# A one-core perceiver block: reordering the stretch behind the cross attention

## The chip, the cores and the metric

The kernel runs on one core of a Trainium2 chip. The metric is the device time of one execution in microseconds (us); the figure for a version is the median of several runs. The core's engines work side by side, each through its own list of instructions in order, and wait for each other through semaphores: PE multiplies matrices (PEld is its loading of weights), DVE does element-wise work and reductions, ACT does activation functions and copies, POOL does general work and issues some transfers, and SP only issues transfers. Transfers run on 16 DMA engines.

## What is computed

x has 2 batches of 512 tokens with 512 features; the context has 2 batches of 8192 tokens. Three residual blocks follow each other, each on a layer norm of its input:

```python
x = x + xattn(layernorm(x), ctx)     # 16 heads of 32, 8192 context tokens, output product Wo
x = x + window_attn(layernorm(x))    # 16 heads of 32, windows of 7 tokens, product W_proj
h = layernorm(x)                     # 1024 tokens
scores = sigmoid(h @ gate_w.T)       # 16 experts
topk_score, topk_ids = top_k(scores.T, 128)      # each expert picks its 128 best tokens
eo = silu(h[ids] @ gw.T + gb) * (h[ids] @ up_w.T + up_b)      # 2048 wide, by expert
eo = (eo @ down_w.T + down_b) * topk_score
shared = (silu(h @ sh_gate_w.T) * (h @ sh_up_w.T)) @ sh_down_w.T     # 1024 wide
x = x + shared + scatter_add(eo, ids)
```

Everything is in float32, except for some bias and mask factors that are split into three bfloat16 parts.

## The kernel before

Tokens lie in eight tiles of 128 rows (`n` 0 to 7; `b` is the batch, four tiles each). The residual x stays in `x_sb` for the whole kernel. A tile framework places instructions on each engine in an order that it chooses near the program's own, and adds the semaphores. A tile of a pool has a fixed number of buffers (`bufs`); a new tile of the same tag waits until the buffer's last readers are done. Pools opened in a `with` block give their memory back at its end, and a pool opened later in the same place waits for the last user of that memory.

Three stages matter here.

**Cross attention.** A loop over 146 slots handles chunks of 512 context tokens. `load` (SP) brings a chunk into one of four `ctx_t` buffers one slot ahead. In the last two slots only `scores` and `values` are left; there the running sum `acc` over the exponentials is added on DVE (L316). Behind the loop, `finish` for the last group sums `acc` on PE (`sm`, L324), takes the reciprocal (L330) and scales into `qT` on POOL (L332). Then `proj_residual` multiplies by Wo for each token tile (`po`, L92) and DVE adds bias and residual (`prt` L96, `x_sb` L97).

**Window attention.** SP loads three 1 MB tiles of `wqkv` and one of `wproj` into a pool of nine (`load_tile`, L371). `layernorm_stats` takes the statistics of all eight token tiles (L68, L69), then a square root on ACT (L71) and a reciprocal; each tile is normalized (`xn`, L77), transposed on PE (`tp`, L85) and copied by ACT into `xnT` (L86). After this, 8 groups (batch, four heads) of five query blocks run as a software pipeline of 40 items: `softmaxed` of one item, one of five `pieces` for the next group (`project` for k, `latent_k`, `project` for q, for v, `latent_v`), then `turned`, `weighed` and `placed` of the items before. A batch's last item is followed by `proj_residual` with W_proj for its four tiles.

**Feed-forward.** Behind that stand, in program order: `pick`, a selector of expert rows (three casts, L582); statistics, normalization, the write of each tile of h to memory (`h_dram`, on SP's queue, L602), transposes into `hT`; the gate product `pg` (L610) and its sigmoid; the selection, 16 rounds of `max`, `max_index` and `match_replace` on DVE (L624 to L627), eight tokens per expert and round; the splitting of the biases into three bfloat16 parts (`raw`, `part`, `bias3`, L641 to L645); and the shared expert, per batch 8 pairs of products `pf` (L658) with silu on ACT and a multiplication into `sT` on DVE (L665), then four products `pso` (L669) and the residual (L674). Then the selected tokens' numbers are transposed (`pt`, L679), `gather` fetches the first expert's tokens from `h_dram` by an indirect transfer on POOL's queue (L687), and 16 experts stream 12 MB of weights each through the nine-tile pool (`pf` L704, `py` L722).

Of the kernel before, what the change touches and what calls it, by code (L numbers as in the profile page):

```python
# [43 lines left out]
def perceiver_kernel(  # L44
# [18 lines left out]
    def layernorm_stats(pool):  # L63

        mv = pool.tile([P, NT, 2], F32, name="mv")
        for n in range(NT):
            st = pool.tile([P, 6], F32, name="st")
            nc.vector.bn_stats(out=st, in_=x_sb[:, n, :])  # L68
            nc.vector.bn_aggr(out=mv[:, n, :], in_=st)  # L69
        sd = pool.tile([P, NT], F32, name="sd")  # L70
        nc.scalar.activation(sd, mv[:, :, 1], AF.Sqrt, bias=eps)  # L71
        rs = pool.tile([P, NT], F32, name="rs")
        nc.vector.reciprocal(rs, sd)
        return mv, rs
# [13 lines left out]
    def proj_residual(aT, w_sb, b_bc, n, ps, pool):  # L88

        po = ps.tile([P, D], F32, tag="ps", name="po")  # L90
        for c in range(DC):
            nc.tensor.matmul(  # L92
                po, lhsT=aT[:, c, ts(n, P)], rhs=w_sb[:, c, :], start=(c == 0), stop=(c == DC - 1)
            )
        t = pool.tile([P, D], F32, tag="row", name="prt")
        nc.vector.tensor_tensor(t, po, b_bc, ALU.add)  # L96
        nc.vector.tensor_tensor(x_sb[:, n, :], x_sb[:, n, :], t, ALU.add)  # L97
# [5 lines left out]
    with ExitStack() as es:  # L103
        cp = es.enter_context(tc.tile_pool(name="a_const", bufs=1))
        tmp = es.enter_context(tc.tile_pool(name="a_tmp", bufs=2))
        ctxp = es.enter_context(tc.tile_pool(name="a_ctx", bufs=4))
# [229 lines left out]
        for slot in range(NS + LAG):  # L336
            if slot + 1 < NS + NKC:
                load(slot + 1)
            s = slot - LAG
# [17 lines left out]
        for i in range(4):  # L357
            finish(len(units) - 1, i)

        wo_sb = load_w(wo, ctxp, "ctx")  # L360
        bo_b = cp.tile([P, D], F32, tag="bv_b", name="bo_b")
        nc.gpsimd.dma_start(out=bo_b, in_=bo.partition_broadcast(P))
        for n in range(NT):
            proj_residual(qT, wo_sb, bo_b, n, ps, tmp)


    wpool = ctx.enter_context(tc.tile_pool(name="w", bufs=9))

    def load_tile(src):
        t = wpool.tile([P, 4, 512], F32, tag="w", name="wt")  # L370
        nc.sync.dma_start(out=t, in_=src)  # L371
        return t


    with ExitStack() as es:
# [3 lines left out]
        ps = es.enter_context(tc.tile_pool(name="b_ps", bufs=8, space=PSUM))  # L379

        wqkv_t = [
            load_tile(wqkv[:, ts(i, D)].rearrange("(c p) f -> p c f", p=P)) for i in range(3)
        ]
        wproj_sb = load_tile(wproj.rearrange("(c p) f -> p c f", p=P))
        bqkv_c = cp.tile([P, 12], F32, name="bqkv_c")
# [25 lines left out]
        xnT = cp.tile([P, DC, T], F32, name="xnT")  # L411
        mv, rs = layernorm_stats(tmp)
        for n in range(NT):
            xn = tmp.tile([P, D], F32, tag="row", name="xn")
            normalized(xn, n, mv, rs)
            transposed(xnT[:, :, ts(n, P)], xn, ps)

        aT = cp.tile([P, G, T], F32, name="aT")
# [8 lines left out]
        def project(i, which):  # L427
# [5 lines left out]
            for c in range(DC):  # L433
                nc.tensor.matmul(  # L434
                    pq, lhsT=wqkv_t[which][:, c, ts(g, P)], rhs=xnT[:, c, ts(b, S)],
# [105 lines left out]
        def placed(i, n):  # L541
# [6 lines left out]
            nc.scalar.copy(aT[:, g, ds(b * S + q0, nq)], tp[:, 0:nq])  # L548
            if g == G - 1 and n == NBQ - 1:
                for m in range(NT // B):  # L550
                    proj_residual(aT, wproj_sb, bproj_b, b * (NT // B) + m, ps, tmp)
# [4 lines left out]
        ]  # L556
        for f in pieces:
            f(0)
# [9 lines left out]


    cp = ctx.enter_context(tc.tile_pool(name="c_const", bufs=1))  # L570
    tmp = ctx.enter_context(tc.tile_pool(name="c_tmp", bufs=2))
    ps = ctx.enter_context(tc.tile_pool(name="c_ps", bufs=8, space=PSUM))
    dram = ctx.enter_context(tc.tile_pool(name="c_dram", bufs=1, space=bass.MemoryType.DRAM))
    h_dram = dram.tile([T, D], F32, name="h_dram")
# [3 lines left out]
    KB3 = 96  # L578
    pick = cp.tile([KB3, E, P], BF16, name="pick")
    for i in range(3):  # L580
        r = ds(32 * i, 32)
        nc.vector.tensor_copy(  # L582
            pick[r], ident[r, ds(32 * i, E)].unsqueeze(2).to_broadcast([32, E, P])
        )
    FB = 2 * F + D
    bias3 = cp.tile([KB3, FB], BF16, name="bias3")

    gate_sb = cp.tile([P, DC, E], F32, name="gate_sb")
    nc.gpsimd.dma_start(out=gate_sb, in_=gate.rearrange("(c p) e -> p c e", p=P))
    idx = cp.tile([P, E], U32, name="idx")  # L590
    scol = cp.tile([P, E], F32, name="scol")

    with ExitStack() as es:
        sp = es.enter_context(tc.tile_pool(name="s_const", bufs=1))
        st = es.enter_context(tc.tile_pool(name="s_tmp", bufs=2))

        hT = sp.tile([P, DC, T], F32, name="hT")
        mv, rs = layernorm_stats(st)
        for n in range(NT):
            h = st.tile([P, D], F32, name="h")  # L600
            normalized(h, n, mv, rs)
            nc.sync.dma_start(out=h_dram[ts(n, P), :], in_=h)  # L602
            transposed(hT[:, :, ts(n, P)], h, ps)


        sc = sp.tile([E, T], F32, name="sc")
        for i in range(T // 512):
            pg = ps.tile([P, 512], F32, tag="ps", name="pg")
            for c in range(DC):
                nc.tensor.matmul(  # L610
                    pg[0:E, :], lhsT=gate_sb[:, c, :], rhs=hT[:, c, ts(i, 512)],
                    start=(c == 0), stop=(c == DC - 1),
                )
            nc.scalar.activation(sc[:, ts(i, 512)], pg[0:E, :], AF.Sigmoid)
# [3 lines left out]
        work = [sp.tile([E, T], F32, tag=f"work{i}", name="work") for i in range(2)]  # L618
        top = sp.tile([E, CAP], F32, name="top")
        top_i = sp.tile([E, CAP], U32, name="top_i")  # L620
        cur = sc
        for i in range(CAP // 8):
            m8 = top[:, ts(i, 8)]
            nc.vector.max(out=m8, in_=cur)  # L624
            nc.vector.max_index(out=top_i[:, ts(i, 8)], in_max=m8, in_values=cur)
            if i < CAP // 8 - 1:
                nc.vector.match_replace(  # L627
                    out=work[i % 2], in_to_replace=m8, in_values=cur, imm_value=-1.0
                )
                cur = work[i % 2]  # L630
        top_f = sp.tile([E, CAP], F32, name="top_f")
        nc.vector.tensor_copy(top_f, top_i)

        raw = sp.tile([KB3, FB], F32, name="raw")
        nc.gpsimd.memset(raw, 0.0)
        for i in range(3):
            for src, lo, n in ((gb, 0, F), (up_b, F, F), (down_b, 2 * F, D)):
                nc.scalar.dma_start(out=raw[ds(32 * i, E), ds(lo, n)], in_=src)
        part = sp.tile([KB3, FB], BF16, name="part")
        for i in range(3):  # L640
            nc.vector.tensor_copy(part, raw)  # L641
            r = ds(32 * i, 32)
            nc.vector.tensor_copy(bias3[r], part[r])
            if i < 2:
                nc.vector.tensor_tensor(raw, raw, part, ALU.subtract)  # L645


        shg = [load_tile(sh_g[i]) for i in range(2)]
        shu = [load_tile(sh_u[i]) for i in range(2)]
        shd = [load_tile(sh_d[i]) for i in range(2)]  # L650
        for i in range(T // 512):
            sT = sp.tile([P, SH // P, 512], F32, tag="sT", name="sT")
            for f in range(SH // P):
                pair = []
                for wts in (shg, shu):
                    pf = ps.tile([P, 512], F32, tag="ps", name="pf")
                    for c in range(DC):
                        nc.tensor.matmul(  # L658
                            pf, lhsT=wts[f // 4][:, c, ts(f % 4, P)], rhs=hT[:, c, ts(i, 512)],
                            start=(c == 0), stop=(c == DC - 1),  # L660
                        )
                    pair.append(pf)
                sg = st.tile([P, 512], F32, name="sg")
                nc.scalar.activation(sg, pair[0], AF.Silu)
                nc.vector.tensor_tensor(sT[:, f, :], pair[1], sg, ALU.mult)  # L665
            for j in range(4):
                po = ps.tile([P, D], F32, tag="ps", name="pso")
                for f in range(SH // P):
                    nc.tensor.matmul(  # L669
                        po, lhsT=sT[:, f, ts(j, P)], rhs=shd[f // 4][:, f % 4, :],  # L670
                        start=(f == 0), stop=(f == SH // P - 1),
                    )
                n = i * 4 + j
                nc.vector.tensor_tensor(x_sb[:, n, :], x_sb[:, n, :], po, ALU.add)  # L674
                nc.sync.dma_start(out=out[ts(n, P), :], in_=x_sb[:, n, :])

        for src, dst in ((top_f, idx), (top, scol)):
# [130 lines left out]
```

## Time and profile before

| | |
|---|---|
| median of 3 runs | 3922.88 us (3919.61 to 3925.23) |
| the profiled execution | 3923.6 us, of which its span in the trace 3921.8 us |
| PE busy | 3822.6 us, 97% of the span |
| DVE busy | 2314.8 us, 59% |
| ACT busy | 1586.1 us, 40% |
| POOL busy | 2059.3 us, 53% |
| DMA, mean | 112 GB/s |

The stages in the trace, in us from the span's start: cross attention ends with its last `av` product at about 2704.5; Wo and the preparation of the window attention last until the first `plv` product (L472) at 2764.1; the window attention's last W_proj product ends at 2963.1; the shared expert's last product ends at 3171.9; the first expert begins at 3178.9.

How to read the views: in the slices a digit is a busy share in tenths, and the row PEclk is the clock that PE was granted, in tenths of full speed. A chain of waits gives start, length and the work or wait that held up the end. In a table of windows each engine has its busy time and, in brackets, its number of instructions; behind them stand the granted clock, the DMA share and GB/s. A row of the timeline has start, length, engine, line, operation, operands and, in square brackets, the idle time before it and what ended it.

### The profile page before, as it was taken

What the parts mean: (1) busy time and instruction counts of PE and PEld (TensorE: products, weight loads), DVE (VectorE), ACT (ScalarE), POOL (GpSimd) and SP (SyncE); (2) the same over time, 40 slices, a digit from 0 to 9 for tenths busy, and PEclk for the clock granted to TensorE, in tenths of its full rate; (3) what the DMA queues carried; (4) which work ended last, traced back from release to release, by engine and by line L of the source; (5) the groups of instructions that cost most, each with busy time, mean ns of one, the idle gap of its engine ahead of it and who ended that gap; (6) DMA issues with size and microseconds to landing.
All of it is one profiled execution on the core that took longest, in us unless ns stands there. A gap on an engine that the chain in (4) does not pass through costs nothing.

```text
span 3921.8 us, 99604 instructions
## 1 busy us (share of the span) xinstructions
PE 3822.6 (97%) x42828; PEld 1891.4 (48%) x42828; DVE 2314.8 (59%) x5833; ACT 1586.1 (40%) x2799; POOL 2059.3 (53%) x512
## 2 busy tenths in 40 slices
PE   7999999999999999999999999999997999999999
PEld 3445554554554554555555455444563444444444
DVE  4887777777777777777777777898346400000000
ACT  1005555555555555555555555675441001111110
POOL 0008998998998998999899899300000000000000
PEclk9889999999999999999999999999997999999999
DMA  4322222222223442222222222220201058888885
GB/s 157 95 84 71 70 70 66 69 69 69 69 69 106 125 125 92 69 69 69 69 69 69 69 69 66 66 85 26 81 33 42 32 203 286 288 288 288 283 285 178
DMA packets 144154, 440.29 MB, mean 112 GB/s; under 512 B 9312, under 2 KB 9456, under 8 KB 118272
## 3 DMA queue, kind: packets, MB, share of 16 engines
q1 hardware_dynamic: 139152, 423.72, 32.9%
q0 software_dynamic: 4272, 9.32, 1.0%
q8 instruction: 335, 5.49, 0.6%
q10 hardware_dynamic: 288, 0.89, 0.1%
q14 instruction: 107, 0.88, 0.1%
HBM read 425.44 MB, written 8.45 MB: 111 GB/s over the span
## 4 chain that ended last, share of the span: by engine, by line
PE 86%; DVE 3%; issue 2%; ACT 1%; DMA 1%; POOLq 0%; DVEq 0%; SPq 0%; ACTq 0%
PE av L304 12%; PE sx L246 12%; PE sc L282 11%; PE pv L226 11%; PE pf L704 11%; PE pk L210 10%; PE py L722 5%; PE sc L288 3%; PE pqkv L434 2%; PE pf L658 2%; PE po L92 1%; PE pso L669 1%; DVE junk L251 1%; PE pow L529 1%; PE tp L85 1%
## 5 line engine op out<-in xcount | busy, mean ns | idle before, releaser
L316 POOL TENSOR_TENSOR acc<-acc,pt 128x2048 f32<-128x2048 f32 x437 | 1992.1, 4558 | 483.9 <-ACT pt L295 482.7
L251 DVE CUSTOM_DVE_ANT_0 junk<-sx,mk 128x512 bf16<-128x512 f32 x2048 | 1416.2, 692 | 610.8 <-PE sx L246 378.1
L295 ACT ACTIVATE pt<-sc,mbias 128x512 f32<-128x512 f32 x2016 | 1218.5, 689 | 952.9 <-PE sc L288 951.4
L246 PE MATMUL sx<-kt,qT 32*128 32x512 f32 x4096 | 651.8, 645 | 0.6 <-ACT kt L214 0.6
L282 PE MATMUL sc<-qT,kt 32*128 32x512 f32 x4096 | 546.7, 594 | 0.0
L304 PE MATMUL av<-pt,vt 128*32 128x512 f32 x4032 | 540.5, 605 | 2.8 <-DVE mst L251 2.8
L226 PEld LDWEIGHTS pv<-wv_sb,ctx_t 128*32 128x32 f32 x16384 | 457.5, 110 | 155.5 <-DVE mst L251 104.4
L210 PE MATMUL pk<-ctx_t,wk_sb 128*32 128x256 f32 x8192 | 506.2, 389 | 2.1 <-DVE mst L251 2.1
L226 PE MATMUL pv<-wv_sb,ctx_t 128*32 128x128 f32 x16384 | 495.0, 273 | 1.3 <-DVE avs L312 1.3
L704 PE MATMUL pf<-wt,xinT 128*128 128x512 f32 x1024 | 461.0, 595 | 1.1
L210 PEld LDWEIGHTS pk<-ctx_t,wk_sb 128*32 128x32 f32 x8192 | 265.7, 112 | 309.0 <-DVE mst L251 133.6
L312 DVE TENSOR_TENSOR avs<-av,avs 128x512 f32<-128x512 f32 x504 | 345.3, 685 | 2.8 <-PE av L304 2.5
L282 PEld LDWEIGHTS sc<-qT,kt 32*128 32x128 f32 x4096 | 245.6, 184 | 202.0 <-issue 160.1
L711 DVE TENSOR_TENSOR eo<-pf,sg 128x512 f32<-128x512 f32 x64 | 44.3, 692 | 468.9 <-PE pf L704 461.9
L704 PEld LDWEIGHTS pf<-wt,xinT 128*128 128x128 f32 x1024 | 193.6, 190 | 222.4 <-issue 214.0
L246 PEld LDWEIGHTS sx<-kt,qT 32*128 32x128 f32 x4096 | 190.6, 185 | 211.4 <-DVE mst L251 159.7
L687 POOL DMA_INDIRECT xin<-h_dram,idx x16 | 15.9, 994 | 496.8 <-PE tp L85 291.7
L728 POOL DMA_INDIRECT out_x<-y,idx x16 | 25.3, 1580 | 408.8 <-DVE y L727 408.8
L304 PEld LDWEIGHTS av<-pt,vt 128*32 128x32 f32 x4032 | 81.6, 108 | 325.9 <-DVE mst L251 281.0
L214 ACT ACTIVATE kt<-pk,bk_c 128x256 f32<-128x256 f32 x256 | 121.2, 473 | 275.0 <-PE pk L210 274.9
L722 PE MATMUL py<-wt,eoT 128*128 128x512 f32 x512 | 222.4, 592 | 0.0
L709 ACT ACTIVATE sg<-pf 128x512 f32<-128x512 f32 x64 | 38.2, 597 | 422.2 <-PE pf L704 422.2
(152 smaller groups left out, 2276.9 us busy)
## 6 DMA issues: line engine op xcount, KB each, us to landing
ctx_t<-in_ctxT SPq DMA_DIRECT2D x160, 1024.0 KB, 6.5
wt<-in_gw SPq DMA_DIRECT2D x64, 1024.0 KB, 5.0
wt<-in_up SPq DMA_DIRECT2D x64, 1024.0 KB, 4.9
wt<-in_down SPq DMA_DIRECT2D x64, 1024.0 KB, 6.6
mk<-mrow SPq DMA_DIRECT2D x128, 256.0 KB, 3.5
wt<-in_wqkv SPq DMA_DIRECT2D x3, 1024.0 KB, 10.4
x_sb<-in_x SPq DMA_DIRECT2D x1, 2048.0 KB, 10.6
wt<-in_sh_g SPq DMA_DIRECT2D x2, 1024.0 KB, 15.1
```

The lines of the kernel that those rows point to most:

```text
L210: nc.tensor.matmul(pk[ts(h, DK), :], lhsT=wk_sb[:, c, ds(g * P + h * DK, DK)], rhs=ctx_t[slot, b][:, c, hs], start=(c == 0), stop=(c == DC ...
L214: nc.scalar.activation(k_t[slot][:, hs], pk, AF.Identity, bias=bk_c[:, g : g + 1])
L226: nc.tensor.matmul(pv[ts(k, DK), i, :], lhsT=ctx_t[slot, b][:, c, ds((2 * half + i) * P + k * DK, DK)], rhs=wv_sb[:, c, ts(g, P)], start=( ...
L246: nc.tensor.matmul(sm, lhsT=qT[r, g, ds(b * S + c * P, P)], rhs=k_t[s][r, :], start=True, stop=True)
L251: nc.vector.tensor_tensor_reduce(out=junk, in0=ss[h], in1=mk_t[s], scale=1.0, scalar=-3.0e38, op0=ALU.add, op1=ALU.max, accum_out=mst[u][: ...
L282: nc.tensor.matmul(sc, lhsT=k_t[s][r, ts(ch, P)], rhs=qT[r, g, ts(b, S)], start=True, stop=False)
L295: nc.scalar.activation(pt[:, h, :], ss[h], AF.Exp, bias=mbias[:, b, cc : cc + 1], scale=SCALE)
L304: nc.tensor.matmul(av[ts(h, DK), :], lhsT=v_t[s][:, ch, ts(h, DK)], rhs=pt_t[s, ch][:, h, :], start=True, stop=True,)
L312: nc.vector.tensor_tensor(avs[u], av, avs[u], ALU.add)
L316: eng.tensor_tensor(acc[u], acc[u], pt_t[s, ch], ALU.add)
L704: nc.tensor.matmul(pf, lhsT=xinT[:, c, :], rhs=wt[:, c, :], start=False, stop=(c == DC - 1))
L722: nc.tensor.matmul(py, lhsT=eoT[:, fq * 4 + c, :], rhs=wt[:, c, :], start=False, stop=(fq == FQ - 1 and c == 3),)
```

## The change

The four-buffer pool of the context chunks (`ctxp`) is opened at the top and lives to the end. In slot 143, the last one that uses a context chunk, SP also loads Wo and the three `wqkv` tiles into its buffers. The nine-tile weight pool becomes those four buffers and a pool of five, taken in turn by a counter; `wproj` and four tiles of the shared expert are requested ahead of the window attention, two more after it.

`finish` of the last group is called after the second Wo tile. `layernorm_stats` takes a range of tokens. The first batch's statistics follow its four Wo tiles, and only its four tiles are transposed before the window attention starts; the second batch's statistics and transposes, the three casts of `pick`, the splitting of the biases (in three loads of up to 2048 columns), and the first batch's layer norm and transposes for the feed-forward are put beside single items of the window attention's pipeline (`at`). `xnT`, `aT` and `hT` become tiles by batch in a pool of three. The writes of `h_dram` and the loads of `raw` go through POOL's queue, which before were SP's and ACT's.

In the shared expert, the second batch's layer norm and transposes stand behind products 1 to 4 of the first batch, the gate products behind product 5, and a round of the selection behind each later product (two behind each `pso`). The transposes `pt` and the gather stay at the end.

```diff
+    ctxp = ctx.enter_context(tc.tile_pool(name="ctx", bufs=4))
+    lnp = ctx.enter_context(tc.tile_pool(name="ln", bufs=2))
-    def layernorm_stats(pool):
+    def layernorm_stats(pool, tokens=range(NT)):
...
-        ctxp = es.enter_context(tc.tile_pool(name="a_ctx", bufs=4))
...
             if slot + 1 < NS + NKC:
                 load(slot + 1)
+            elif slot + 1 == NS + NKC:
+                wo_sb = load_w(wo, ctxp, "ctx")
+                wqkv_t = [load_w(wqkv[:, ts(i, D)], ctxp, "ctx") for i in range(3)]
...
         values(*waiting)
-        for i in range(4):
-            finish(len(units) - 1, i)
-
-        wo_sb = load_w(wo, ctxp, "ctx")
...
         for n in range(NT):
             proj_residual(qT, wo_sb, bo_b, n, ps, tmp)
+            if n == 1:
+                for i in range(4):
+                    finish(len(units) - 1, i)
+            if n == NT // B - 1:
+                ln_b0 = layernorm_stats(lnp, range(NT // B))
-    wpool = ctx.enter_context(tc.tile_pool(name="w", bufs=9))
+    wpool = ctx.enter_context(tc.tile_pool(name="w", bufs=5))
+    loads = [4]
 
     def load_tile(src):
-        t = wpool.tile([P, 4, 512], F32, tag="w", name="wt")
+        pool, tag = ((ctxp, "ctx"), (wpool, "w"))[loads[0] % 9 >= 4]
+        loads[0] += 1
+        t = pool.tile([P, 4, 512], F32, tag=tag, name="wt")
         nc.sync.dma_start(out=t, in_=src)
         return t
...
+        def bias_in(src, n):
+            raw = bp.tile([KB3, F], F32, name="raw")
+            nc.gpsimd.memset(raw, 0.0)
+            for i in range(3):
+                nc.gpsimd.dma_start(out=raw[ds(32 * i, E), 0:n], in_=src)
+            raws.append(raw)
+
+        def bias_part(i, lo, n):
+            raw = raws[-1]
+            part = bp.tile([KB3, F], BF16, name="part")
+            nc.vector.tensor_copy(part[:, 0:n], raw[:, 0:n])
+            r = ds(32 * i, 32)
+            nc.vector.tensor_copy(bias3[r, ds(lo, n)], part[r, 0:n])
+            if i < 2:
+                nc.vector.tensor_tensor(raw[:, 0:n], raw[:, 0:n], part[:, 0:n], ALU.subtract)
+
+        def forward_in(n, key):
+
+            b, m = divmod(n, NT // B)
+            if m == 0:
+                hT[b] = batch_tile("hT")
+            h = ctmp.tile([P, D], F32, name="h")
+            normalized(h, n, *lns[key])
+            nc.gpsimd.dma_start(out=h_dram[ts(n, P), :], in_=h)
+            transposed(hT[b][:, :, ts(m, P)], h, ps)
+
+        lns, raws = {"b0": ln_b0}, []
+        at(2, norm, 1, "b1")
+        for i, k in enumerate((4, 6, 8, 10)):
+            at(k, lambda n: attention_in(n, lns["b1"]), NT // B + i)
+        for i in range(3):
+            at(3 + 2 * i, picks, i)
+        k = 9
+        for src, lo, n in ((gb, 0, F), (up_b, F, F), (down_b, 2 * F, D)):
+            at(k, bias_in, src, n)
+            for i in range(3):
+                k += 2
+                at(k, bias_part, i, lo, n)
+        at(29, norm, 0, "f0")
+        for i, k in enumerate((31, 33, 35, 37)):
+            at(k, forward_in, i, "f0")
+        for n in range(NT // B):
+            attention_in(n, ln_b0)
         for f in pieces:
             f(0)
         for k in range(len(items) + 3):
...
+            for f in beside.get(k, ()):
+                f()
...
+    norm(1, "f1")
+    for b in range(B):
...
+            if b == 0 and 1 <= f <= 4:
+                forward_in(NT // B + f - 1, "f1")
+            elif b == 0 and f == 5:
+                gated(0)
+                gated(1)
+            elif b == 1 or f > 5:
+                select()
+        for j in range(4):
...
+            select()
+            select()
```

## What the prediction was, before the result

> **What bounds the kernel now.** I read the slices of the page first: they say where PE, busy for 97% of the span, is not.
>
> ```profile
> PE   7999999999999999999999999999997999999999
> DVE  4887777777777777777777777898346400000000
> PEclk9889999999999999999999999999997999999999
> ```
>
> PE dips, with its clock, in slice 30 of 40; the stretch that the change touches begins in slice 27, where DVE too is disturbed. So the second view is the chain of waits over that stretch.
>
> ```profile
> 2708.78 27.68 PE po L92 x64
> 2737.31 0.59 DVE x_sb L97
> 2738.44 10.36 DMA wt<-in_wqkv
> 2748.94 5.38 PE pqkv L434 x8
> ...
> 2964.47 5.47 DVE pick L582
> ...
> 2985.18 9.03 PE pg L610 x16
> ...
> 3037.87 0.61 DVE sT L665
> ...
> 3089.50 54.93 PE pf L658 x128
> 3144.43 27.47 PE pso L669 x64
> 3172.14 6.72 issue
> ```
>
> Work of PE is left four times here: for the `wqkv` load, for DVE ahead of `pg`, for one `sT` product on DVE, and at the end for the gather. Third, the windows of these stages, for idle time and clock.
>
> ```profile
> 2704.50:2764.10 59.60, 48.18 (x131) 22.27 (x130) 30.75 (x54) 9.78 (x16) 8.37 (x18) 0.94 0.43 156
> 2764.10:2861.10 97.00, 95.83 (x632) 61.03 (x633) 37.68 (x291) 53.62 (x153) 0.54 (x4) 1.00 0.02 6
> 2926.00:2963.10 37.10, 35.01 (x150) 22.62 (x148) 14.55 (x70) 10.30 (x34) 0.00 (x0) 0.68 0.00 0
> ...
> 2963.10:2974.60 11.50, 0.00 (x0) 0.00 (x0) 10.93 (x10) 1.58 (x2) 4.74 (x2) 0.60 0.36 117
> 2974.60:2985.10 10.50, 8.16 (x32) 6.00 (x32) 3.64 (x7) 4.10 (x7) 0.00 (x0) 0.50 0.59 203
> ...
> 3028.70:3038.50 9.80, 0.03 (x1) 0.00 (x0) 9.74 (x12) 0.00 (x0) 0.00 (x0) 0.75 0.00 0
> ```
>
> The window attention (second row) is PE's: 95.8 of 97 us, at full clock, DVE 39% busy, ACT 55%. Behind it PE has nothing for 11.5 us, then transposes at half clock for 10.5 us, and later nothing for 9.8 us.
>
> Last, single durations from the timeline.
>
> ```profile
> 2923.97 0.54 PE L517 MATMUL tpw<-ident,sb 103*109 103x103 f32 x4
> 2931.64 1.06 PE L517 MATMUL tpw<-ident,sb 103*109 103x103 f32 x4
> ...
> 2964.47 7.93 DVE L582 CAST pick<-ident 32x2048 bf16<-32x2048 f32 x3
> 2969.31 1.28 ACT L71 ACT_TABLE_LOAD   x1 [22.17 <-POOL raw L635]
> ...
> 3009.58 4.93 DVE L645 TENSOR_TENSOR raw<-raw,part 96x4608 f32<-96x4608 f32 x1
> ```
>
> Four transposes take 0.54 us at full and 1.06 us at half clock. The three casts of `pick` are 7.9 us of DVE.
>
> **The change part by part.** The order is that of the changed kernel's built lists of instructions; up to the last `av` and from the first expert on, PE's list is the old one.
>
> *A. Wo to the first group.* Before, PE waits from 2704.5 to 2707.7 for the last `acc`, and after `po` (to 2736.5) 12.4 us pass with transposes and two waits until `pqkv` at 2748.9. Now PE has two `po` tiles, `sm`, six `po` tiles, 16 transposes (of batch 0 only), `pqkv`. `po` can start at 2704.5 and ends after 27.7 + 1.1 (`sm`) at 2733.3. The chain behind `sm` (copy 0.6, reciprocals 3.4, POOL's `qT` product 1.3) takes about 6 us with DVE's queue, and tiles 2 and 3 cover 6.9 us. On POOL a clearing of `raw` (3.95 us for 4608 columns, so 1.8 for 2048) and three issues now stand ahead of that product; they can begin at 2707.6 and are over at about 2711, 6 us before it is due. `wqkv` is loaded in a slot with idle DMA: nothing. The loads of `wlat_bd` behind POOL's `qT` product leave 18 us earlier than before. SP's next load waits for the last `po`, and `wproj` behind it has 100 us.
>
> DVE is the tight one. A `po` tile costs it 2.36 us (`prt` to aggregate), eight 18.9; with reciprocals 3.4, a first bias part and subtraction that the framework put here (1.1 + 2.2) and two `xn` (1.0), it has 26.6 us from 2708.2 to the last `prt`, which by its queue ends at 2734.3. The transposes then go at the pace of `xn`, to 2737.6; the copy to `xnT` 0.6; `pqkv` starts at 2738.4: **10.5 us earlier**. Now DVE has the three casts (7.9), two `xn` (1.1) and 6.6 us of bias work queued ahead of the `ext` copies that `plv` needs: it is through at 2752.8. ACT delivers that `ext` at 2753.4 (before: 2763.9). So 0.6 us to spare; bounds 0 to +3 if single operations are longer here.
>
> *B. The window attention*, 199.0 us from `plv` to the last W_proj product, gets eight tiles of transposes from the idle stretches. They are PE's own time: six at 0.54 and two, in the tail, at 1.06, together +5.4. DVE gets 15 us more: the other bias parts (9.5 + 2.4), `xn` and `h` (3.3). What hides it is the pipeline: between an item's `sw` and its `tpw` PE has at least 6.9 us of other work by the timeline (an item with a projection 5.2, the next one's `sw` 0.6 and `pl` 1.1), and DVE and ACT need 2.7 of it (maxima and scaling 1.2, exponentials 1.2, hand-overs 0.3), so 4.2 us are free; the longest new block on DVE is 3.9 us (1.1 + 0.6 + 2.2). Cost 0; without the cover at most the whole 15. The loads of `raw` on POOL's queue wait for DVE's earlier part and DVE waits for them; two items (8 us) lie between and memset, issue and landing take about 6. Cost 0, bound 2. The writes of `h_dram` leave SP for POOL, behind which only `vt`'s clearing stands (0.13 us, an item ahead): 0.
>
> The first batch's square root falls between exponentials. The trace has a table load at each such switch, 1.28 us, so 2.6 us more on ACT. Behind the first W_proj tiles PE has 6.0 us of work up to `plv`; ACT goes exponentials (to 4.8), load (6.1), root (6.4), `ext` (7.1), DVE's copies (7.5): `plv` is **1.5 us** late. [...] The trace shows the load, [...] so I take 1.5; bounds 0 and 5.
>
> The clock of the tail is the second place. From 2927.6 it is half, though PE counts as busy for 35.0 of 37.1 us; the last projections are over there. [...] two tiles at 1.06, as taken. If any work of PE counted, the tail would run at full clock, worth 9 us (below).
>
> *C. W_proj's end to the last `pso`*, 208.8 us before. Now `pf` follows W_proj at once (its `hT` is ready), and PE's list adds up to: `pf` 2 x 55.1, `pso` 2 x 27.5, gate products 6.9 (x16 at the rate of `pf`, x128 in 55.1), four tiles of transposes 2.2: 174.3. **34.5 less**: 11.5 idle, 8.3 of the transposes, 2.1 of `pg`'s half clock, 9.8 of DVE's jam, 2.8 of slow clock after it. The layer norm of batch 1 (3.7 us behind the last `po`) has two pairs of `pf` (13.7 us) over it. The selection, 16 rounds of 3.7 us, starts 50 us in and shares DVE with products of 0.7 us: it is over near 117 of 174. Eight PSUM buffers bridge its longest block (7.3 us) ahead of an `sT`.
>
> *D. The gather* still waits for transposes behind the last `pso`: its 7.0 us stay. The experts: 0.
>
> Sum: -10.5 + 5.4 + 1.5 - 34.5 = -38.1. Against the profiled execution's 3923.6 us (span 3921.8, 1.8 around it) 3885.5; that execution is 0.7 over the median of 3922.88, so **3885 us**.
>
> **The rivals.** *DVE's new work comes through (R1).* For it: DVE and ACT are in order, and the free 4.2 us are hardly more than the 3.9 us block. Against: 39% busy. Half of the 15 us makes 3892, all of it 3900.
> *The tail keeps its clock (R2).* For it: one trace doesn't show how much work keeps the clock, and the tail gets more of it. [...] Five items become bound by ACT (2.0) instead of PE (3.1), W_proj's last four tiles take 13.8 for 16.3, the transposes 1.0 less: 9 us, 3876.
> *The weights' two pools (R3, slower).* 3178.9 to the end is 743 us, PE 733 busy with DMA at 0.80: the stage with least cover. If the turn between the two pools were off so that a load waits for a tile used just before, each load shows part of its 5 us. It decides at 38 us, 0.2 us for each of 192 tiles; with 1.6 us (landing 5.0 less one tile's 3.4) for the 4 in 9 tiles in `ctxp`, 85 tiles, +136: about 4021. Against: the counter starts at 4, and the built waits name the tile nine loads back, as before.
> *The reordering does nothing in effect (R4):* the framework restores the old order, about 3922. The built lists speak against it.
>
> **How the numbers follow.** My forecast 0.70 (3880 to 3890), R1 0.14, R2 0.11, R3 0.03, R4 0.02. Range 3876 to 3897: it takes in R2's value, A's and B's upper bounds and the nearer part of R1. A difference of 0.2% (8 us) is about what can be told from none. Faster 0.95, same 0.02, slower 0.03.
>
> **What would show it.** Right: `pqkv` starts about 34 us after the last `av`, not 44; no DVE step in the chain between W_proj and `pf`; the stretch from W_proj's end to the last `pso` near 174 us at clock 1.00; half clock once, in the tail; the 7 us ahead of the first expert unchanged. Wrong: waits of `tpw` for ACT or of `plv` for DVE in the window attention of more than 5 us together (R1), a clock near 1.00 in the tail (R2), or `pf` L704's successor waiting for `wt` loads (R3).

## The result and the profile after

The changed kernel takes 3876.49 us (median of 4 runs, 3875.93 to 3878.32) against 3921.54 us of the kernel before (4 runs, 3919.61 to 3925.23): a ratio of 0.9881, 95% interval 0.9866 to 0.9896 (the two medians alone give 0.9885). That is 45 us less, where 38 were forecast. The profiled execution took 3878.3 us, its span is 3876.5 us.

The slices of the page, PE, DVE and the granted clock. The dip of PE and PEclk in slice 30 (counted from 0) is gone. DVE's work has moved forward: slice 28, Wo and the first groups, has 7 instead of 3, and slice 30 has 3 instead of 6.

```profile
PE   7999999999999999999999999999999999999998
DVE  4877777777777777777777777799743600000000
PEclk9889999999999999999999999999999999999999
```

The chain of waits over the stretch that the change touches (start, length, what):

```profile
2706.97 7.06 PE po L99 x16
2714.03 1.00 PE sm L330 x8
2715.03 20.81 PE po L99 x48
2735.86 0.70 DVE prt L103
...
2740.35 3.71 PE pqkv L471 x8
...
2935.28 16.46 PE po L99 x32
2951.74 8.58 PE pf L716 x20
```

`po` follows the last `av` at once, the sum `sm` stands behind two Wo tiles, the wait for the `wqkv` load is gone (`pqkv` starts 33.4 us after the last `av`; it was 44.4), and `pf` follows W_proj without any step of DVE between them.

The windows by stage (us; busy time and instructions of PE, PEld, DVE, ACT, POOL; granted clock, DMA share, GB/s):

```profile
2706.97:2753.80 46.83, 42.92 (x114) 18.58 (x114) 42.91 (x64) 7.59 (x13) 16.10 (x27) 1.00 0.45 151
2753.80:2853.45 99.65, 98.02 (x649) 62.94 (x650) 53.12 (x310) 55.85 (x157) 3.79 (x8) 1.00 0.03 6
...
2915.00:2951.74 36.74, 36.06 (x217) 23.75 (x216) 18.19 (x92) 15.83 (x47) 0.54 (x1) 0.86 0.11 37
2951.74:3125.48 173.74, 173.74 (x418) 75.78 (x417) 76.95 (x111) 17.21 (x26) 2.15 (x4) 1.00 0.14 52
3125.48:3132.30 6.82, 0.21 (x3) 0.14 (x3) 0.85 (x3) 0.00 (x0) 2.02 (x2) 0.71 0.86 305
```

The fourth row is the shared expert: PE busy for all of 173.7 us at full clock. The last row is the gather, unchanged. The third row is the tail of the window attention: its clock is 0.86, not 0.68 as before.

By stage, from the profiled executions (us):

| stage | before | after | difference | forecast |
|---|---|---|---|---|
| to the last `av` | 2704.5 | 2707.0 | +2.5 | 0 |
| A, last `av` to first `plv` | 59.6 | 46.8 | -12.8 | -10.5 |
| B, to W_proj's end | 199.0 | 197.9 | -1.1 | +6.9 |
| C, to the last `pso` | 208.8 | 173.7 | -35.1 | -34.5 |
| D, gather | 7.0 | 6.8 | -0.2 | 0 |
| experts | 742.9 | 744.2 | +1.3 | 0 |

The first row is not put down to the change: PE's list is the old one there, and counted by products the two executions are 2.4 us apart after 300 us of start-up and still 2.4 us apart at the end of the loop. Over the profiled executions of all thirteen kernels the last `av` ends anywhere from 2704.0 to 2709.4 us. The question that the experiments had to settle is B: 8 us better than its sum.

### The profile page after: what moved, and what is told of

Same layout as the page of the kernel before. It is cut to its first block, busy times and chain, and to the rows that moved or that the text cites. A ratio compares the mean times of both kernels' runs of the same rounds, so it can differ in the third digit from the quotient of the medians.

```text
span 3876.5 us, 99601 instructions
## 1 busy us (share of the span) xinstructions
PE 3807.9 (98%) x42828; PEld 1883.3 (49%) x42828; DVE 2314.5 (60%) x5851; ACT 1589.1 (41%) x2804; POOL 2069.1 (53%) x531
## 4 chain that ended last, share of the span: by engine, by line
PE 88%; DVE 2%; issue 1%; ACT 1%; DMA 0%; POOLq 0%; DVEq 0%; ACTq 0%
PE av L310 13%; PE sx L252 12%; PE sc L288 12%; PE pv L232 11%; PE pf L775 11%; PE pk L216 10%; PE py L793 5%; PE pf L716 3%; PE sc L294 3%; PE pqkv L471 2%; PE po L99 1%; PE pso L734 1%; DVE junk L257 1%; PE tp L91 1%; PE pow L566 1%
```

## Experiments

Stages are named as in the table. Variants e1 to e8 start from the changed kernel, b10 to b12 from the kernel before.

**e1: no transposes of h in the tail.** The tail is what follows the last projection product.

```diff
-        at(29, norm, 0, "f0")
-        for i, k in enumerate((31, 33, 35, 37)):
+        at(25, norm, 0, "f0")
+        for i, k in enumerate((27, 29, 31, 33)):
```

> The first batch's layer norm for the feed-forward and its four tiles of transposes (tp of h) stand beside items 25 to 33 instead of 29 to 37, so that the tail of the window attention (from the last projection product plv to W_proj) has none of them. Theory 1 [...]: with none in the tail the half clock begins 3.4 to 6.8 us after the last plv, not 11 to 12 us after it as in the changed kernel, and lasts 17 to 24 us instead of 10; the stretch from plv to W_proj's end grows from 198 to 202-205 us and the time from 3876.5 to about 3880-3883 us. Theory 2 (they do not count, as the prediction had it; the later half clock of the changed kernel comes from where the clock's windows happen to fall, or from the shorter items): half clock still about 11 us after the last plv, 3875-3878 us.

Measured: 3884.6 us (profiled execution 3879.6, the others 3884.3 to 3885.4), 0.9905 of before (0.9889 to 0.9922). The half clock lasts 20.5 us instead of 10.2, and B takes 202.8 us instead of 197.9. By the stage that is theory 1, by which the transposes keep the clock up. The total is 1.6 us above its range; the three executions that were not profiled are 5 us longer than the profiled one, and which stage takes that is not known.

In the traces of both kernels the half-clock stretches start, and all but the last one end, on one grid with a step of 3.41 us (in the changed kernel 2930.34 and 3128.31 lie 58 steps apart, in the kernel before 2740.10 and 2927.83 lie 55), so the windows below are cut along that grid; these two lists end with the step in which the clock is half. First the changed kernel:

```profile
2920.10:2923.51 3.41, 3.41 (x38) 2.89 (x36) 2.26 (x20) 2.79 (x9) 0.00 (x0) 1.00 0.00 0
2923.51:2926.93 3.42, 3.25 (x39) 2.70 (x39) 2.51 (x20) 2.98 (x12) 0.00 (x0) 1.00 0.02 5
2926.93:2930.34 3.41, 3.37 (x33) 2.74 (x32) 2.10 (x16) 3.06 (x11) 0.00 (x0) 1.00 0.01 2
2930.34:2933.75 3.41, 3.41 (x19) 2.94 (x19) 0.66 (x3) 1.61 (x6) 0.00 (x0) 0.50 0.00 0
```

and e1:

```profile
2913.78:2917.19 3.41, 3.41 (x40) 3.14 (x39) 2.41 (x18) 2.15 (x7) 0.00 (x0) 1.00 0.79 288
2917.19:2920.60 3.41, 3.16 (x42) 2.67 (x41) 2.63 (x21) 2.73 (x10) 0.00 (x0) 1.00 0.05 19
2920.60:2924.01 3.41, 3.41 (x20) 2.65 (x20) 1.41 (x11) 1.84 (x7) 0.00 (x0) 0.50 0.00 0
```

In both, the clock falls behind the first window that has neither a product of the projections nor a tile of h's transposes. In the changed kernel two windows more (2920.10 and 2923.51) hold such a tile, 0.44 us each. PE's busy share doesn't tell the two kinds apart: behind 3.37 of 3.41 us the clock fell, behind 3.25 it stayed.

**e2: all four tiles in the tail.**

```diff
-        for i, k in enumerate((31, 33, 35, 37)):
+        for i, k in enumerate((35, 37, 39, 41)):
```

> The same four tiles of transposes stand beside items 35, 37, 39 and 41, all in the tail. Theory 1 (they count): no 3.4 us of the tail is without one, so the half clock goes away or shrinks to one window; W_proj's last four tiles take 13.8 us instead of 16.5, the items keep their full-clock pace, less 1.2 us for two more copies on ACT, which bounds the tail: about 3872-3874 us. Theory 2 (they do not count): half clock as in the changed kernel or longer, and the transposes are paid at half clock (1.06 instead of 0.44 us): 3877-3880 us.

Measured: 3871.6 us, 0.9872 (0.9855 to 0.9888). B takes 193.5 us, and from the last `av` to the gather no half clock is left. The last windows of the tail:

```profile
2917.93:2921.34 3.41, 3.16 (x38) 2.50 (x37) 2.49 (x16) 2.77 (x9) 0.54 (x1) 1.00 0.19 74
2921.34:2924.76 3.42, 3.25 (x35) 2.80 (x35) 2.53 (x20) 3.00 (x11) 0.54 (x1) 1.00 0.03 7
2924.76:2928.17 3.41, 2.90 (x35) 2.54 (x33) 2.00 (x14) 3.02 (x12) 0.00 (x0) 1.00 0.21 79
2928.17:2931.58 3.41, 3.28 (x27) 2.57 (x26) 0.95 (x4) 2.36 (x8) 0.00 (x0) 1.00 0.00 0
```

PE is idle for half a microsecond of the third (2.90 of 3.41 us busy), and the clock stays at 1.00: here too the busy share doesn't decide it, and each of these windows has its four transposes. The time is 0.4 us better than theory 1's range. W_proj's last four tiles take 13.8 us.

**e8: smaller transposes.** To e1 are added, beside items 35, 37, 39 and 41, four transposes each of the window attention's own size.

```diff
+        def more():
+            tp = ps.tile([P, 4, P], F32, tag="ps", name="tpm")
+            for c in range(4):
+                nc.tensor.transpose(
+                    tp[0:BQ, c, 0:BQ], hT[0][0:BQ, c, 0:BQ], ident[0:BQ, 0:BQ]
+                )
...
+        for k in (35, 37, 39, 41):
+            at(k, more)
```

> The kernel with h's transposes early (half clock 20.5 us long in the tail) gets four more transposes of 103 x 103, of the window attention's own size, beside each of the items 35, 37, 39 and 41; their results are not used. Theory 1 (what holds the clock is the amount of dense work in a window of 3.4 us, and the tail's items alone are just short of it): these hold it as the 128 x 128 ones did, no half clock in the tail, and W_proj's end comes about 5 us earlier in spite of 1.5 us more work: about 3874-3878 us beside 3882-3884. Theory 2 (only transposes that fill all 128 rows count, and the window attention's own transposes do not): half clock as without them, and the added transposes cost up to 3 us: 3883-3888 us.

Measured: 3880.4 us, 0.9892 (0.9876 to 0.9907), B 198.9 us, half clock 10.2 us. Neither number of theory 1 or 2 came out, but the windows speak for theory 1. Behind the two that have the added transposes the clock stays at 1.00; the framework had moved the third set behind the next window, which has none, and behind it the clock falls to 0.50:

```profile
2917.99:2921.41 3.42, 3.42 (x42) 2.84 (x41) 2.41 (x20) 2.75 (x10) 0.00 (x0) 1.00 0.03 12
2921.41:2924.82 3.41, 3.41 (x44) 3.02 (x43) 2.25 (x18) 2.35 (x10) 0.00 (x0) 1.00 0.00 0
2924.82:2928.23 3.41, 3.18 (x36) 2.42 (x32) 2.37 (x20) 2.92 (x11) 0.00 (x0) 1.00 0.02 5
2928.24:2931.65 3.41, 3.41 (x23) 3.41 (x22) 0.60 (x3) 2.23 (x7) 0.00 (x0) 0.50 0.01 2
```

So here transposes of 103 rows kept it at 1.00 as well.

**e4: more work on DVE in the window attention** (rival R1 and the slack of 4.2 us).

```diff
-            nc.vector.tensor_copy(part[:, 0:n], raw[:, 0:n])
+            for _ in range(3):
+                nc.vector.tensor_copy(part[:, 0:n], raw[:, 0:n])
...
-            nc.vector.tensor_copy(bias3[r, ds(lo, n)], part[r, 0:n])
+            for _ in range(2):
+                nc.vector.tensor_copy(bias3[r, ds(lo, n)], part[r, 0:n])
```

> In every step of the bias splitting the cast into part is made three times and the copy into bias3 twice, with the same result: the long steps on DVE beside the window attention grow from 3.9 to 6.9 us (two of them from 1.8 to 4.8), some 19 us of DVE in all. Theory 1 (the prediction's slack of 4.2 us an item): four steps outlast it by 2.7 us and two by 0.6, so plv to W_proj's end grows from 198 to about 210 us, and the time to about 3888 us. Theory 2 (rival: DVE's work spreads over several items, and the pipeline holds more than one item's slack): under 3 us, 3876-3879 us. Theory 3 (R1 of the prediction: no cover at all): all of it, about 3895 us.

Measured: 3877.1 us, 0.9886 (0.9870 to 0.9903). B is 197.1 us, A 47.7 (0.9 more, in PE's waits for DVE ahead of the first group: 1.5 and 1.3 us instead of 0.9 and 1.0). DVE works 18 us more from Wo on, of which 14 in B; they cost nothing that shows in B and 0.9 us in A. Theory 2: the slack of 4.2 us an item was too careful, and R1 is out.

**e6: the wqkv loads back behind Wo.**

```diff
-                wqkv_t = [load_w(wqkv[:, ts(i, D)], ctxp, "ctx") for i in range(3)]
...
+        wqkv_t = [
+            load_tile(wqkv[:, ts(i, D)].rearrange("(c p) f -> p c f", p=P)) for i in range(3)
+        ]
         wproj_sb = load_tile(wproj.rearrange("(c p) f -> p c f", p=P))
```

> Only the three loads of wqkv go back behind the Wo stage, into the pool whose memory is that of the closed cross attention; Wo keeps its early load, and everything else is as changed. Theory 1 (the prediction's part A: most of it is the load's wait): pqkv starts some 12 us behind the last po as before, not 4.5, so 8 us come back, and with the pause one or two windows of half clock, worth 1.7 each: 3884-3888 us. Theory 2 (the gain of A is that of fewer transposes and statistics ahead of the first group, and the load would have been hidden): under 3 us, 3876-3879 us.

Measured: 3887.9 us, 0.9908 (0.9893 to 0.9923). A takes 57.0 us, 10.1 more than in the changed kernel. Its chain of waits:

```profile
2714.45 20.81 PE po L99 x48
...
2737.20 10.34 DMA wt<-in_wqkv
2747.53 0.14 issue
2747.67 5.97 PE pqkv L473 x8
```

The load is back on the path, and with the pause 10.2 us of half clock, which makes the first `pqkv` 5.97 us instead of 3.71. Theory 1.

**b12: only the sum behind two Wo tiles, in the kernel before.**

```diff
-        for i in range(4):
-            finish(len(units) - 1, i)
...
             proj_residual(qT, wo_sb, bo_b, n, ps, tmp)
+            if n == 1:
+                for i in range(4):
+                    finish(len(units) - 1, i)
```

> The kernel before, with finish of the last group called behind the second Wo tile, and nothing else. Theory 1 (prediction, part A: PE's wait for acc of 3.2 us is hidden by two Wo tiles): 3.2 us less from the last av to the last po; behind it the wait for the wqkv load, which starts when the last po is done, moves with it: total 3918.5-3920 us. Theory 2 (the load of wqkv is bound to something that does not move, so the 3.2 us turn into a longer wait there): no change, 3921-3923 us.

Measured: 3919.9 us, 0.9991 (0.9984 to 0.9998) of 3924.0. A takes 56.8 us instead of 59.6. The 3.2 us without PE ahead of `sm` are gone; the wait for the load stays. The total alone would not carry this; the stage does.

**e7: the second batch's layer norm and the gate products ahead of the shared expert.**

```diff
     norm(1, "f1")
+    for n in range(NT // B, NT):
+        forward_in(n, "f1")
+    gated(0)
+    gated(1)
     for b in range(B):
...
-            if b == 0 and 1 <= f <= 4:
-                forward_in(NT // B + f - 1, "f1")
-            elif b == 0 and f == 5:
-                gated(0)
-                gated(1)
-            elif b == 1 or f > 5:
+            if b == 1 or f > 5:
                 select()
```

> The second batch's layer norm, its four tiles of transposes and both gate products stand ahead of the shared expert again; the first batch's norm, the casts of pick and the biases stay beside the window attention. Theory 1 (part C: PE has nothing while the norm is made, and then a slow clock): some 4.6 us of norm and 2.8 us of transposes at DVE's pace without PE, and transposes and gate products at half clock worth about 3 to 5 us, so that W_proj's end to the last pso grows from 173.7 to 183-187 us and the time to 3886-3890 us. Theory 2 (the gain of C lies in what DVE no longer does ahead of the norm, picks and biases): under 4 us, at most 3880 us.

Measured: 3883.7 us (profiled execution 3888.0), 0.9899 (0.9884 to 0.9914). C is 182.8 us, 9.1 more: nearly theory 1's 183 to 187, while the median lies 2.3 us under the time it gave. From the timeline of PE:

```profile
2957.07 1.94 PE L91 MATMUL tp<-ident,h 128*128 128x128 f32 x8 [3.67 <-DVE h L83]
2960.25 1.97 PE L91 MATMUL tp<-ident,h 128*128 128x128 f32 x8 [1.24 <-DVE h L83]
2962.15 9.04 PE L679 MATMUL pg<-hT,gate_sb 128*16 128x512 f32 x16
```

4.9 us without PE; the transposes and the first gate products run at half clock (10.2 us of it, from 2955.97 to 2966.21).

**b11: the kernel before without the splitting of the biases.** The loads and the clearing of `raw` go with it, and the experts have no bias.

```diff
+    nc.gpsimd.memset(bias3, 0.0)
...
-        for i in range(3):
-            nc.vector.tensor_copy(part, raw)
-            r = ds(32 * i, 32)
-            nc.vector.tensor_copy(bias3[r], part[r])
-            if i < 2:
-                nc.vector.tensor_tensor(raw, raw, part, ALU.subtract)
```

> The kernel before, with the splitting of the biases left out (bias3 is cleared instead, so the experts have no bias). Theory 1 (prediction, part C: the 9.8 us in which PE waits for one sT product, and the slow clock behind it, come from the 25 us that the splitting puts into DVE's queue): the gap ahead of pf goes, 10 to 13 us less: 3909-3913 us. Theory 2 (the selection alone, 58 us, holds the sT products up): the gap stays, or most of it: 3918-3923 us.

Measured: 3911.7 us, 0.9967 (0.9956 to 0.9979) of 3924.0. C is 196.4 us, 12.4 less; the gap of 9.8 us and the half clock behind it are gone, though the 58 us of selection are all still there. The 12 us without PE behind W_proj stay. Theory 1.

**b10: the kernel before with the casts of pick elsewhere.** `pick` gets a pool of its own that opens ahead of the window attention, and the casts stand beside items 3, 5 and 7; in the trace they run ahead of the first group, from 2736.7 us on.

```diff
+    pkp = ctx.enter_context(tc.tile_pool(name="pk", bufs=1))
+    pick = pkp.tile([KB3, E, P], BF16, name="pick")
...
+            if k in (3, 5, 7):
+                r = ds(16 * (k - 3), 32)
+                nc.vector.tensor_copy(
+                    pick[r], ident[r, ds(16 * (k - 3), E)].unsqueeze(2).to_broadcast([32, E, P])
+                )
```

> The kernel before, with one edit: the three casts of pick (7.9 us of DVE) no longer stand behind W_proj; the framework puts them into the preparation of the window attention, behind the last prt. Theory 1 (the casts are what holds the layer norm up: the chain showed pick between W_proj and the gate product): the 11.5 us without PE behind W_proj shrink by 5 to 7.9, and 1 or 2 us of slow clock with them. Ahead of the window attention the load of wqkv, 10.4 us long, covers most of the casts, so 0 to 4 us are paid there: total 3913 to 3918 us. Theory 2 (the norm's own chain of statistics, root, xn and transposes is the bound, and the casts only fill its gaps): under 2 us less, 3920-3923 us.

Measured: 3920.2 us, 0.9990 (0.9981 to 0.9998) of 3924.0. C is 208.3 us against 208.8, and the total is in theory 2's range; yet theory 1's mechanism is there. Three windows: behind W_proj, the gate products, and ahead of `pf`:

```profile
2960.12:2966.34 6.22, 0.01 (x1) 0.04 (x1) 5.68 (x7) 0.30 (x1) 4.77 (x2) 0.91 0.53 174
2967.37:2986.80 19.43, 15.94 (x45) 6.68 (x43) 3.28 (x6) 6.55 (x10) 0.00 (x0) 0.62 0.39 133
3021.61:3035.14 13.53, 0.01 (x1) 0.01 (x1) 13.47 (x14) 0.00 (x0) 0.00 (x0) 0.68 0.00 0
```

The first pause of PE shrank from 11.5 to 6.2 us, and the second, with DVE busy for all of it, grew from 9.8 to 13.5. The gate products end 4.2 us earlier behind W_proj. But in DVE's list selection and splitting stand ahead of the first `sT` product, which ends up 43.6 us behind the gate products before and 47.3 here, and the trace shows why: the framework put seven rounds of the selection ahead of it instead of six, and a round takes 3.7 us. So the gain is given back in DVE's queue. What the casts give with six rounds was not run. Of the 6.2 us that are left of the first pause, 2.5 are a first `h` that lasts 3.1 us instead of 0.55 beside POOL's clearing of `raw` (last section).

**e3: the gather earlier.** The last round of the selection is over before the second batch's seventh pair; `pt`, the index and the first gather follow that pair.

```diff
+            elif b == 1 and f == 6:
+                top_f = sp.tile([E, CAP], F32, name="top_f")
+                nc.vector.tensor_copy(top_f, top_i)
+                for src, dst in ((top_f, idx), (top, scol)):
+                    pt = ps.tile([P, E], F32, tag="ps", name="pt")
+                    nc.tensor.transpose(pt, src, ident[0:E, 0:E])
+                    nc.vector.tensor_copy(dst, pt)
+                xin0 = ctmp.tile([P, D], F32, tag="h", name="xin")
+                nc.gpsimd.indirect_dma_start(
+                    out=xin0, out_offset=None, in_=h_dram,
+                    in_offset=bass.IndirectOffsetOnAxis(ap=idx[:, 0:1], axis=0),
+                )
             elif b == 1 or f > 5:
...
-        xin = ep.tile([P, D], F32, name="xin")
+        if e < 1:
+            return xin0
+        xin = ctmp.tile([P, D], F32, tag="h", name="xin")
...
```

> The selection is over by the second batch's sixth pair of pf; the transposes of its result (pt), the index and the first expert's gather follow its seventh pair instead of the last pso. Theory 1 (the gather is the only thing that the first expert waits for): the 6.6 us without work of PE ahead of the first expert shrink to about 0.7 (one copy of the transposed tokens), and with the pause goes the half clock behind it (10.2 us long, worth 5.1): about 3865 us. Theory 2 (the weights of the first expert come late once the pause is gone, since they arrive at a DMA share of 0.8): half of it or less, 3870-3876 us, with pf of the experts waiting for weight loads.

Measured: 3867.8 us, 0.9864 (0.9847 to 0.9880). Its chain ahead of the experts:

```profile
3089.43 7.07 PE pf L716 x16
3096.50 27.46 PE pso L746 x64
3123.97 0.44 PE tp L91 x4
3124.40 0.86 PE pf L778 x4
```

The first expert follows the last `pso` without a pause, and no half clock comes behind it. The experts' stage shortens from 744.2 to 740.9 us, PE's busy time in it from 733.4 to 730.0: by that the half clock was worth 3.3 us, not the 5.1 expected. Theory 1, with this one term too large.

**e5: e2 and e3 together.**

> The late transposes (items 35 to 41) and the early gather together. If the two gains are of separate causes they add: -4.9 and -8.7 us from the changed kernel's 3876.5, about 3863 us, with no half clock anywhere between the cross attention and the end. If the early gather lives on the later arrival of W_proj, or the weights of the experts become the bound, the sum falls short: 3866-3868 us.

Measured: 3863.8 us (5 runs, 3861.2 to 3866.1), 0.9847 (0.9833 to 0.9860). The two gains add. From the last `av` on, the clock is halved only in the last 7 us of the execution. This version is ahead of both kernels: 12.7 us less than the changed one by the medians.

## Why the prediction was right and where it failed

The direction was right, three of the four parts came out within 2.5 us, and the total lies 8.5 us below the forecast and close to the value of rival R2. It is under the 3880 to 3890 us of the forecast itself, and only 0.5 us inside the whole range, whose lower end was R2's value. Part B was 8.0 us better than its sum and A 2.3; the start and the experts, put at 0, came out 3.8 us longer; that this brings the total nearer to the forecast is luck. Point by point.

*A, -10.5 forecast, -12.8 measured.* The two causes are as told: the sum behind two Wo tiles is 2.8 us of it (b12), the earlier load 10.1 (e6). `pqkv` came 0.5 us earlier than worked out. What the sum left out is the clock: before, two half-clock stretches of 3.4 us lay between the last `po` and `plv`, the second of them in `pqkv`. They went with the pause, which shortens `pqkv` to `plv` by 1.7 us (15.2 to 13.5). Part C had counted such a term, part A had not. DVE's casts and bias parts made no wait: PE waits 1.0 us for `ext` ahead of the first `plv`, as before. They had more room than worked out, since the term for the casts was twice too large: they take 1.2 us each here, 3.6 together, not 7.9. In the kernel before the first of them lasted 5.5 us, beside POOL's clearing of `raw`, and the other two 1.2 each. (A slip of the working: 26.6 us from 2708.2 on make 2734.8, not 2734.3; it decides nothing.)

*B, +6.9 forecast, -1.1 measured.* Up to the tail the sum holds: +4.4 us for +4.7. The square root cost what the trace had said:

```profile
2870.06 1.21 ACT L543 ACTIVATE sb<-sb,nm 103x109 f32<-103x109 f32 x4 [16.34 <-DVE nm L541]
2871.30 1.28 ACT L77 ACT_TABLE_LOAD   x1
2872.59 0.30 ACT L77 ACTIVATE sd<-mv,eps 128x4 f32<-128x4 f32 x1
2872.79 0.67 ACT L487 ACTIVATE ext<-pqkv,bqkv_c 128x512 f32<-128x512 f32 x1
```

The exponential ends at 2871.27, the load begins at 2871.30 and the root follows it at once; the load takes 1.28 us, and `plv` came 1.1 us late (forecast 1.5).

The step that failed is the tail: "two tiles at 1.06, as taken", with the clock at half from its start. From the first `tpw` behind the last `plv` to W_proj's end the tail took 39.1 us before and takes 33.7 now, two tiles included: -5.4 where +2.1 was in the sum. These 7.5 us are nearly all of B's miss. Part of them is luck: in the three variants of the kernel before, the tail took 36.5 to 37.6 us, so by an estimate from these times up to 2.6 us lie in which execution the forecast had. The step rested on the assumption that transposes do not keep the clock up, which no trace of this case had shown. Here they do: taking them out of the tail brings 20.5 us of half clock (e1), putting all of them in leaves none (e2). The changed kernel itself shows it ahead of the first group, in one window of the 3.41 us grid:

```profile
2735.78:2739.19 3.41, 1.94 (x15) 1.45 (x15) 3.21 (x7) 1.60 (x4) 0.80 (x1) 1.00 0.69 199
2739.19:2742.61 3.42, 2.75 (x10) 1.31 (x10) 3.36 (x6) 0.84 (x3) 0.00 (x0) 1.00 0.98 303
```

In the first of them PE does nothing but transposes and the end of a Wo product, and is idle for 1.5 of 3.4 us; the clock is whole in the second. The trace of the kernel before had shown it too, where PE did nothing but transposes:

```profile
2740.14 6.25 PE L85 MATMUL tp<-ident,xn 128*128 128x128 f32 x32 [3.70 <-DVE xn L77]
...
2740.10:2743.51 3.41, 3.37 (x16) 3.00 (x16) 1.93 (x4) 1.66 (x3) 2.65 (x6) 0.50 0.91 298
2743.51:2746.93 3.42, 2.68 (x18) 1.68 (x16) 1.80 (x4) 2.89 (x6) 0.86 (x3) 1.00 1.15 379
```

The clock is half in the first window, which has sixteen transposes and nothing else, and whole in the second. So the forecast's assumption stood against rows that were at hand. The row that it gave for it doesn't support it: that PE is busy for 35.0 of 37.1 us in a tail at a mean clock of 0.68 says that busy time doesn't decide, but not that transposes don't.

*R2* was thus right in its mechanism and for most of its size: 7.5 of its 9 us, in which the luck above is included. Its sign, a clock near 1.00 in the tail, did not come (0.86). The rest is the half clock that is left, 10.2 us in the last items and in W_proj (16.5 us instead of 13.8); e2 gains that too.

*R1* is out: e4's 14 us more on DVE in the window attention left B as it was, and of its sign, more than 5 us of waits, there are 2.5 us of `plv` for DVE and 0.2 of `tpw` for ACT. *R3* did not happen: the experts' stage has 0.7 us more of PE work, and a half clock of 10.2 instead of 6.8 us at its start. *R4* is out by the result.

*C, -34.5 forecast, -35.1 measured.* PE is busy for all of it, as listed. Two causes are shown apart: norm, transposes and gate products out of the way are 9.1 us (e7), the splitting off DVE 12.4 (b11). The casts alone gave 0.5 us, with one more round of the selection ahead of `sT` (b10). How the remaining 13.6 us divide between the casts, the first batch's norm and transposes, and what only all of it together gives, was not tried.

*D* stayed at 6.8 us, as forecast; e3 shows that it need not.

## What to carry to other kernels

A clock that halves was a cost of its own here: with 20.5, 10.2 and 0 us of half clock in the tail, B took 202.8, 197.9 and 193.5 us (e1, the changed kernel, e2). Look for it even where PE counts as busy, and try there the work that has to be done anyhow, before adding any. When a pause ahead of a stage is removed, ask which engine limits the stage behind it, and look at the order in its queue: a pause can come back there as a longer wait (b10). And take a long chain of a slow engine off the end of a stage as soon as its input is there (the gather), instead of where the program reads best.

## What the runs showed of the hardware

PE's busy share of a step of 3.41 us did not tell whether the clock stayed. In the changed kernel it fell behind the step from 2926.93, with 3.37 us of PE, and stayed behind those from 2923.51 with 3.25 and from 2735.78 with 1.94; in e2 it stayed behind 2.90 us (from 2924.76), in the kernel before it fell behind 3.16 (from 2924.42):

```profile
2924.42:2927.83 3.41, 3.16 (x40) 2.54 (x39) 2.38 (x18) 2.56 (x10) 0.00 (x0) 1.00 0.29 120
2927.83:2931.24 3.41, 3.41 (x18) 2.85 (x21) 1.23 (x11) 2.05 (x9) 0.00 (x0) 0.50 0.00 0
```

Both steps of the tail behind which it fell hold only `tpw`, `pow`, `tpo` and `sw` (31 such products begin in the changed kernel's, 37 in the other); four full transposes more, 0.44 us, stand in each of the steps from 2920.10 and 2923.51, behind which it stayed. The gate products, with 16 active columns each, ran at 1.00 too (7.0 us of them from 2994.69 in the changed kernel). What in a step decides is not shown.

The kernel before had 23.9 us of half clock in its tail (2927.83 to 2951.73) and took 199.0 us in B; b10, which leaves the tail alone, took 197.4. The changed kernel had 10.2 (2930.34 to 2940.58). By the timelines its last four W_proj tiles took 16.7 us, in e3, e4 and e7, which leave its tail alone too, 16.6 to 16.7, and at full clock, in e2, 13.9.

Beside a clearing on POOL single operations of DVE took longer. In b10 (POOL's own row first):

```profile
2961.95 3.96 POOL L636 MEMSET raw<- 96x4608 f32 x1
2963.12 3.52 DVE L77 TENSOR_SCALAR h<-x_sb,mv,rs 128x512 f32<-128x512 f32 x2
```

The first of these two `h` ends at 2966.19, 0.3 us behind the clearing's end; it lasts 3.1 us, later ones 0.55. In the kernel before it is the first cast of `pick` that lasts 5.5 us, until 2969.95, beside a clearing that ends at 2968.87. A cast alone takes 1.2 us in the changed kernel and in b10. Why is not shown by these runs.
